# One attention and FFN block on one core: the rows of x are made again from their normalised form, and two kinds of transfer change queues

## The chip, the cores and the metric

The kernel runs on one core of a Trainium2 chip. The metric is device microseconds of one execution, the median of several runs. Before the change: median 1097.92 us of 3 runs, 1096.86 to 1098.83.

The engines are named as the profile names them: PE (TensorE, matrix products), DVE (VectorE), ACT (ScalarE), POOL (GpSimd) and SP (SyncE). SP computes nothing: it only issues transfers (DMAs). ACT and POOL can issue transfers too. Each engine works through its own instructions in the order in which the program gives them; one that waits holds up all that is behind it on that engine.

## The reference

```python
def attention(x, Wq, Wk, Wv, Wo):
    q, k, v = x @ Wq, x @ Wk, x @ Wv
    qT, kT, vT = (swapaxes(a, 1, 2) for a in (q, k, v))
    weights = softmax(qT @ swapaxes(kT, 1, 2) / sqrt(16))
    return swapaxes(weights @ vT, 1, 2) @ Wo

def ffn(x, lut, gate_idx, up_idx, down_idx):
    gate, up = x @ lut[gate_idx].T, x @ lut[up_idx].T
    return (silu(gate) * up) @ lut[down_idx].T

x = x + attention(layernorm(x), Wq, Wk, Wv, Wo)
x = x + ffn(layernorm(x), lut, gate_idx, up_idx, down_idx)
```

x is 2 x 2048 x 512, float32. The attention is over the 512 channels, not over the positions, so its weights are 512 x 512 for each of the two batches. The FFN's inner width is 1376; its three weights are indices into a table of 16 numbers. The layer norms have neither scale nor shift.

## The kernel before

The 4096 rows are cut into 8 chunks c of 512 rows, each into 4 blocks j of 128 rows (32 blocks k in all). A chunk of x lies in SBUF as tile `x{c}`, 128 partitions x 4 blocks x 512 channels, 1 MB. The order of work on PE, ACT, DVE and SP is the order in which the program is written out; helpers interleave the stages by hand.

1. Gram stage, up to 79.7 us. For each block, DVE computes the statistics (`stats`, L147), ACT takes the root (`sqrt`, L163), DVE the rest (`rest`), ACT writes the normalised block into a tile `xn` (`pair`, `normed`, L199), and PE adds its Gram matrix to `gp` (L396). `xn` holds two blocks and has two buffers. The normalised rows are also stored in DRAM as `nd`: chunks 3 to 7 from the `xn` pairs (`store`, L196, 10 stores of 512 KB), chunks 0 to 2 by a second pass of ACT into tiles `n` (`n_stored`, L493, 12 stores of 256 KB), which runs beside the Gram products of chunks 3, 5 and 6. SP issues all of them, and between them the loads of the weights wk and wq (L361, 1 MB each).
2. Small products, 79.7 to 176 us: the 512 x 512 matrices of the attention, with the softmax; they end in a matrix m for each batch.
3. The y stage, 176 to 289.5 us, one block k after the other (`y_product`, L709, 3.43 us each on PE). The rows needed for it are reloaded from `nd` in a turned layout (`n_load`, L688) and turned by DVE (`n_turned`, nT, L693). `side(k)` does what follows one product: `added(k-1)` adds y to x (L716), with sums on ACT (L158, L159); at a chunk's end the finished chunk of x is stored as `x1d` in DRAM (L722, 1 MB). `f_normed(k-6)` writes the second norm's rows into an `xn` pair, which `store` (L196) puts into DRAM as `xnd`. Every fourth block, `f_load` reloads a finished chunk of `xnd` into the room of the old x chunk (4 transfers of 256 KB, L688), and `f_turned(k-14)` lets DVE turn it into `xb` (L693). `f_sums` makes the sums that the fast products need (L128, L131).
4. Gate and up, 289.5 to 823.5 us: 44 units `GateUp(f, p)` of seven products each (L820), with copies by ACT (L849, L855, L860), silu by ACT (L872, L884), and adds by DVE. The last `added`, `f_normed`, turns and sums of stage 3 run here: `late` puts them into the list `todo`, one entry after each product. Between products DVE also looks up the FFN's weights (`pump`), whose indices POOL fetches (L271, L272, L304). The hidden rows are stored as `hd` (L843).
5. Down, 823.5 us to the end: 16 units `Down(h, jj)` of 16.85 us. Each loads its hidden rows (`Hidden`, L976, L982, 2.7 MB per chunk) and its two blocks of x (`r`, from `x1d`, L1018), adds the products to `r` (L131), and stores `r` as the output (L1047, L1085). The copies of products to SBUF are ACT's (L1055, L1062, L1068). A unit is created, and so its loads are issued, one unit ahead.

The index fetches are the only transfers that POOL issues. All others are SP's.

Of the kernel before, what the change touches and what calls it, by code (L numbers as in the profile page):

```python
# [40 lines left out]
F32 = mybir.dt.float32  # L44
# [3 lines left out]
AF = mybir.ActivationFunctionType  # L48
# [6 lines left out]
P = 128  # L55
# [6 lines left out]
def tile_attn_ffn(  # L62
# [13 lines left out]
    nc = tc.nc  # L76
    B, S, E = x.shape
    KB = E // P
    NLUT = lut.shape[1]
    INTER = down_idx.shape[0]  # L80
    J = 4
    CH = J * P
    NCH = B * S // CH
    CPB = S // CH
    NBLK = NCH * J
# [6 lines left out]
    Q = 32  # L92
# [10 lines left out]
    dram = ctx.enter_context(tc.tile_pool(name="dram", bufs=1, space=DRAM))  # L103
# [4 lines left out]
    eps_sb = const.tile([P, 1], F32, tag="eps", name="eps_sb")  # L108
    lut_i = lut_sb.bitcast(I32)
    wd = wdp.tile([P, NFT, E], F32, tag="wd", name="wd")  # L110
    x1d = dram.tile([NCH, P, J, E], F32, tag="x1d", name="x1d")
    nd = dram.tile([NCH, P, KB, J, P], F32, tag="nd", name="nd")
    xnd = dram.tile([NCH, P, KB, J, P], F32, tag="xnd", name="xnd")
    hd = dram.tile([NCH, NFT, P, CH], F32, tag="hd", name="hd")
# [4 lines left out]
    def room(tag, name):  # L119
        return keep.tile([P, J, E], F32, tag=tag, name=name)  # L120
# [11 lines left out]


    class Norm:
        def __init__(self, c, name):
            self.name = f"{name}{c}"
            self.rstd = const.tile([P, J], F32, tag=f"rstd_{self.name}", name=f"rstd_{self.name}")
            self.nmr = const.tile([P, J], F32, tag=f"nmr_{self.name}", name=f"nmr_{self.name}")
            self.minus, self.scale = -1.0, 1.0
# [25 lines left out]
        def rest(self, a, b):  # L165
            r0, q = self.r0[:, a:b], self.q[:, a:b]
            mean, var = self.mv[:, a:b, 0], self.mv[:, a:b, 1]
            rstd, nmr = self.rstd[:, a:b], self.nmr[:, a:b]
            stt = nc.vector.scalar_tensor_tensor
            nc.vector.reciprocal(r0, r0)  # L170

            if self.scale != 1.0:
                nc.vector.tensor_scalar_mul(var, var, self.scale)
            stt(q, var, EPS, r0, ALU.add, ALU.mult)
            stt(q, q, -0.5, r0, ALU.mult, ALU.mult)
            stt(rstd, q, 1.5, r0, ALU.add, ALU.mult)
            stt(nmr, mean, self.minus, rstd, ALU.mult, ALU.mult)

        def pair(self, j, block, quarters=False):


            if j % 2 == 0:
                self.xn = xnp.tile([P, KB, 2, P], F32, tag="xn", name=f"xn_{self.name}_{j}", bufs=2)
            to = self.xn[:, :, j % 2, :]
            if quarters:
                to = to.rearrange("p i (m a) -> p m i a", a=Q)
                block = block.rearrange("p (m i a) -> p m i a", i=KB, a=Q)
            else:
                block = block.rearrange("p (i e) -> p i e", i=KB)
            self.normed(j, block, to)  # L190
            return self.xn

        def store(self, j, dest):

            if j % 2:
                nc.sync.dma_start(dest[:, :, j - 1 : j + 1, :], self.xn)  # L196

        def normed(self, j, block, to):
            nc.scalar.activation(  # L199
# [137 lines left out]
    def pump(us):  # L337

        owed[0] = min(owed[0] + us, 2 * us + 1.0)
        while owed[0] > 0:  # L340
            cost = next(lookup, None)
            if cost is None:
                return
            owed[0] -= cost


    xc = [room(f"x{c}", f"x_{c}") for c in range(NCH)]
# [33 lines left out]


    ln1 = [Norm(c, "a") for c in range(NCH)]
    ln2 = [Norm(c, "f") for c in range(NCH)]
    gp = {}
    STORED = 3

# [101 lines left out]
    def n_stored():  # L489
        c, j = to_store.pop(0)  # L490
        t = sums.tile([P, E], F32, tag="e", name=f"n_{c}_{j}")
        ln1[c].normed(j, xc[c][:, j, :], t)
        nc.sync.dma_start(nd[c][:, :, j, :], t.rearrange("p (i e) -> p i e", i=KB))  # L493

    for c in range(1, NCH):
        for j in range(J):
# [180 lines left out]
    nls, nTs, ys, xfs, fls = {}, {}, {}, {}, {}  # L677
    xb, xs = {}, {}

    def block(k):  # L680
        return xc[k // J][:, k % J, :]

    def reload(t, rows):

        rows = rows.rearrange("(t b) i j e -> i b t (j e)", b=Q)
        t = t.rearrange("p t (j e) -> p t (j e)", e=P)
        for i in range(KB):
            nc.sync.dma_start(t[i * Q : (i + 1) * Q], rows[i])  # L688
        return t.rearrange("p t (j m a) -> p j m t a", j=J, a=Q)

    def turn(to, t):

        nc.vector.transpose(to.rearrange("p m (t b) -> p m t b", b=Q), t)  # L693

    N_AT = ("a0", "a1", "a0", "a1", "a2", "a3", "a1", "a3")

    def n_load(c):
        nls[c] = reload(room(N_AT[c], f"nl_{c}"), nd[c])

    def n_turned(k):  # L700
        if k < NBLK:
# [11 lines left out]
    def added(k):  # L713
        c, j = divmod(k, J)
        total = small.tile([P, 1], F32, tag="total", name=f"total_{k}")
        nc.vector.scalar_tensor_tensor(  # L716
            block(k), ys[k], 1.0, block(k), ALU.mult, ALU.add, accum_out=total
        )
        ln2[c].sums(j, total, block(k))
        if j == J - 1:  # L720
            ln2[c].sqrt(0, J)
            nc.sync.dma_start(x1d[c], xc[c])  # L722

    def f_normed(k):
        c, j = divmod(k, J)
        ln2[c].pair(j, block(k), quarters=True)
        ln2[c].store(j, xnd[c])
# [5 lines left out]
        return xb[c][:, :, j * P : (j + 1) * P]  # L733

    def f_load(c):
        fls[c] = reload(room(f"x{c}", f"fl_{c}"), xnd[c])

    def f_turned(k):
        turn(f_place(k), fls[k // J][:, k % J])
# [30 lines left out]
        [("sq1", 1), (f"x{NCH - 1}", 0), (f"x{NCH - 1}", 1)],  # L770
    ]

    def side(k):

        if k - 1 < NBLK:
            added(k - 1)
        if 0 <= k - 14 < NBLK and k < NBLK:
            f_turned(k - 14)
        if k % J == 1 and 0 <= (k - 5) // J < NCH:
            ln2[(k - 5) // J].rest(0, J)  # L780
        if 0 <= k - 6 < NBLK:
            f_normed(k - 6)
        if k % J == 3 and 0 <= (k - 11) // J < NCH:
            f_load((k - 11) // J)
        if 2 * J + 14 <= k < 2 * J + 18:
            next(f_pairs[0])

    f_pairs = {p: f_sums(p) for p in range(NPR)}
# [5 lines left out]
    for k in range(NBLK):  # L794
        if k:
            n_turned(k + 1)
        y_product(k)
        if k == 0:
            before[0].a4()
            n_turned(1)  # L800
            n_load(1)
        else:
            if k % J == 3 and k // J + 2 < NCH:
                n_load(k // J + 2)
            side(k)
        pump(1.4 if k < 14 else 0.7)
    pps.release()
    sums.release()
    ffn = tc.alloc_tile_pool(name="ffn", bufs=1, reuse_waits="tile")
# [116 lines left out]
            pump(1.0)  # L926


    def late(i, turned=None, pair=None):
        def ops():  # L930
            if i < 8:
                side(NBLK + i)
            if turned is not None:
                f_turned(turned)
            if pair is not None:
                next(f_pairs[pair])

        todo.append(ops)

    what = [dict(turned=k) for k in range(NBLK - 14, 5 * J)] + [dict(pair=1)] * 4  # L940
    what += [dict(turned=k) for k in range(5 * J, 6 * J)] + [dict(pair=2)] * 4
    what += [dict(turned=k) for k in range(6 * J, NBLK)] + [dict(pair=3)] * 4
    for i, w in enumerate(what):
        late(i, **w)

# [61 lines left out]
    class Down:  # L1007


        def __init__(self, h, jj):  # L1010
            self.h, self.c, self.jj, self.name = h, h.c, jj, f"{h.c}_{jj}"
            self.r = []
            if h.c % 2 == 0 and jj == 0:
                for q in range(2):
                    rows_in[q] = room(f"x{1 + q}", f"r_{h.c}_{q}")
            for i, j in enumerate((jj, 2 + jj)):
                t = rows_in[h.c % 2][:, 2 * jj + i, :]
                nc.sync.dma_start(t, x1d[h.c][:, j, :])  # L1018
                self.r.append(t)

        def at(self, a):
            return a[:, self.jj * P : (self.jj + 1) * P]
# [69 lines left out]
        def end(self):  # L1092
            pass

    rows_in = {}

    def by_two(ops):
        return [
# [4 lines left out]
    units = [(0, 0), (1, 0), (0, 1), (0, 2), (0, 3), (1, 1), (1, 2), (1, 3)]  # L1103
    units += [(f, p) for f in range(2, NFT) for p in range(NPR)]
    line = Line(between)
    for f, p in units:
# [3 lines left out]
        if f == NFT - 1 and p == 0:  # L1110
# [3 lines left out]
            for name in ("hp0", "dT"):  # L1114
                hps[name] = tc.alloc_tile_pool(
                    name=name, bufs=1, side="right", reuse_waits="tile"
                )
            hps[0] = hps["hp0"]
            h = Hidden(0)
# [4 lines left out]
        if f == NFT - 1 and p == 3:  # L1124
            units = [Down(h, 0)]
# [9 lines left out]
    for c in range(NCH):  # L1135
        nxt = None
        for jj in range(2):
            if c == 0 and jj == 0:
                line.flush()
                ffn.release()  # L1140
                wgu.release()
                hps[1] = tc.alloc_tile_pool(name="hp1", bufs=1, reuse_waits="tile")
                dtp = tc.alloc_tile_pool(name="dt", bufs=6, reuse_waits="tile")
            if jj == 0 and c + 1 < NCH:
                nxt = Hidden(c + 1)
                nxt.rest_of()
            u = units.pop(0)
            if jj == 0:
                units.append(Down(h, 1))
            elif nxt is not None:  # L1150
                units.append(Down(nxt, 0))
                todo += by_two(nxt.sums())
            line.run(u, final=nxt is None and jj == 1)
        for op in todo:
            op()
        todo.clear()
        h = nxt
# [52 lines left out]
```

## Time and profile before

| what | value |
|---|---|
| median of 3 runs | 1097.92 us |
| the profiled execution: its time | 1099.27 us |
| the profiled execution: its span, first to last instruction | 1096.7 us |
| mean granted clock of PE | 0.998 |
| moved by DMA | 125.51 MB, mean 114 GB/s |
| y stage window, 216 to 262 us | 13.06 MB, 284 GB/s |

The page's part 3 (queue, kind: packets, MB, share of 16 engines' span) and its part 6 (what is moved, by whose queue, how often, KB each, median us from the issue to the landing) tell who moves what:

```profile
q1 hardware_dynamic: 76320, 117.47, 34.1%
q0 software_dynamic: 2240, 7.41, 2.2%
...
nl<-nd SPq DMA_DIRECT2D x32, 256.0 KB, 6.3
x1d<-x SPq DMA_DIRECT2D x8, 1024.0 KB, 9.3
xnd<-xn_f SPq DMA_DIRECT2D x16, 512.0 KB, 6.8
fl<-xnd SPq DMA_DIRECT2D x32, 256.0 KB, 6.8
r<-x1d SPq DMA_DIRECT2D x32, 256.0 KB, 3.9
```

The q1 line is SP's queue; the q0 line is POOL's, with the index fetches alone. In a wait line, the engine and line that waited stand left of the arrow and what ended the wait stands right of it, followed by the us in total, the number of times and the longest.

### The profile page before, as it was taken

What the parts mean: (1) busy time and instruction counts of PE and PEld (TensorE: products, weight loads), DVE (VectorE), ACT (ScalarE), POOL (GpSimd) and SP (SyncE); (2) the same over time, 40 slices, a digit from 0 to 9 for tenths busy, and PEclk for the clock granted to TensorE, in tenths of its full rate; (3) what the DMA queues carried; (4) which work ended last, traced back from release to release, by engine and by line L of the source; (5) the groups of instructions that cost most, each with busy time, mean ns of one, the idle gap of its engine ahead of it and who ended that gap; (6) DMA issues with size and microseconds to landing.
All of it is one profiled execution on the core that took longest, in us unless ns stands there. A gap on an engine that the chain in (4) does not pass through costs nothing.

```text
span 1096.7 us, 10068 instructions
## 1 busy us (share of the span) xinstructions
PE 1086.0 (99%) x3460; PEld 649.2 (59%) x3460; DVE 709.7 (65%) x1340; ACT 295.9 (27%) x554; POOL 15.7 (1%) x34
## 2 busy tenths in 40 slices
PE   9999999999999999999999999999999999999998
PEld 5668886444434444444444444444338888888887
DVE  6977777877665787878888787763553334433341
ACT  4642532554522222222322222222221000000000
POOL 0000000000000000000000000000000000000000
PEclk9999999999999999999999999999999999999999
DMA  8571313799861111111111111111415544345521
GB/s 342 174 233 23 75 39 87 208 285 280 237 178 48 48 62 58 64 48 68 57 61 65 56 67 54 48 48 39 140 55 175 171 151 144 99 156 171 160 68 39
DMA packets 78610, 125.51 MB, mean 114 GB/s; under 512 B 14288, under 2 KB 34000, under 8 KB 76640
## 3 DMA queue, kind: packets, MB, share of 16 engines
q1 hardware_dynamic: 76320, 117.47, 34.1%
q0 software_dynamic: 2240, 7.41, 2.2%
q8 instruction: 27, 0.44, 0.2%
q14 instruction: 23, 0.19, 0.1%
HBM read 68.76 MB, written 56.10 MB: 114 GB/s over the span
## 4 chain that ended last, share of the span: by engine, by line
PE 90%; DMA 4%; DVE 3%; ACT 2%; SPq 1%; issue 1%; ACTq 0%; DVEq 0%
PE a_g L820 27%; PE a_d L820 14%; PE c_g L820 13%; PE c_d L820 7%; PE b_g L820 7%; PE y L709 6%; PE b_d L820 4%; PE gp L396 3%; DMA fl<-xnd 2%; PE ea_t L546 1%; PE ea_p L546 1%; PE ea_m L546 1%; PE ea_s L546 1%; DMA xnd<-xn_f 1%; DMA nd<-xn_a 1%; DVE st_a L147 1%
## 5 line engine op out<-in xcount | busy, mean ns | idle before, releaser
L709 PE MATMUL y<-m,nT 128*128 128x512 f32 x256 | 110.5, 593 | 1.5 <-DVE nT L693 1.5
L131 DVE TENSOR_TENSOR c<-c_g,u 128x512 f32<-128x512 f32 (+1 forms) x44 | 30.4, 690 | 121.0 <-PE c_g L820 110.2
L709 PEld LDWEIGHTS y<-m,nT 128*128 128x128 f32 x256 | 48.5, 190 | 62.4 <-issue 56.9
L820 PE MATMUL a_g<-xb,s 128*128 128x512 f32 (+1 forms) x176 | 82.8, 593 | 0.8 <-DVE c L131 0.8
L820 PE MATMUL a_g<-xb,w 128*128 128x512 f32 (+1 forms) x176 | 82.8, 593 | 0.0
L820 PE MATMUL c_g<-xb,w 128*128 128x512 f32 (+1 forms) x176 | 82.7, 592 | 0.0
L820 PE MATMUL b_g<-xb,w 128*128 128x512 f32 (+1 forms) x176 | 82.7, 592 | 0.0
L820 PE MATMUL a_g<-xT_a,s 128*128 128x512 f32 (+1 forms) x176 | 82.7, 592 | 0.0
L872 ACT ACTIVATE h<-h 128x512 f32<-128x512 f32 (+1 forms) x44 | 27.7, 630 | 163.2 <-DVE h L131 163.2
L396 PE MATMUL gp<-xn_a 128*128 128x512 f32 (+3 forms) x256 | 70.3, 435 | 1.0 <-ACT xn_a L199 1.0
L820 PE MATMUL a_g<-xT_sq,s 128*128 128x512 f32 (+1 forms) x132 | 63.4, 603 | 2.2 <-ACT p L849 2.2
L396 PEld LDWEIGHTS gp<-xn_a 128*128 128x128 f32 x256 | 44.2, 190 | 27.7 <-issue 15.5
L820 PEld LDWEIGHTS a_g<-xb,s 128*128 128x128 f32 (+1 forms) x176 | 32.9, 188 | 43.7 <-issue 37.7
L245 DVE TENSOR_SCALAR gu<-idx_gu,lut_x,lut_sb 128x1024 int32<-128x1024 int32 (+1 forms) x77 | 58.6, 794 | 0.0
L820 PEld LDWEIGHTS a_g<-xb,w 128*128 128x128 f32 (+1 forms) x176 | 32.9, 188 | 42.7 <-issue 42.0
L820 PEld LDWEIGHTS a_g<-xT_a,s 128*128 128x128 f32 (+1 forms) x176 | 33.0, 188 | 42.5 <-issue 42.5
L820 PEld LDWEIGHTS b_g<-xb,w 128*128 128x128 f32 (+1 forms) x176 | 33.0, 188 | 42.5 <-issue 42.5
L820 PEld LDWEIGHTS c_g<-xb,w 128*128 128x128 f32 (+1 forms) x176 | 33.0, 188 | 42.5 <-issue 42.3
L257 DVE COPY_PREDICATED gu<-b_gu,gu 128x1024 f32<-128x1024 int16 (+1 forms) x44 | 56.3, 1280 | 0.8
L820 PE MATMUL a_d<-dT,hs_a 128*128 128x256 f32 x224 | 56.2, 379 | 0.0
L257 DVE COPY_PREDICATED wd<-b_wd,wd 128x512 f32<-128x512 int16 (+2 forms) x63 | 54.1, 859 | 1.1
L131 DVE TENSOR_TENSOR r<-r,a_d 128x256 f32<-128x256 f32 x32 | 13.5, 421 | 54.0 <-PE a_d L820 54.0
(240 smaller groups left out, 1721.3 us busy)
## 6 DMA issues: line engine op xcount, KB each, us to landing
hd<-h SPq DMA_DIRECT2D x80, 256.0 KB, 2.0
h<-hd SPq DMA_DIRECT2D x40, 512.0 KB, 6.5
nl<-nd SPq DMA_DIRECT2D x32, 256.0 KB, 6.3
x1d<-x SPq DMA_DIRECT2D x8, 1024.0 KB, 9.3
xnd<-xn_f SPq DMA_DIRECT2D x16, 512.0 KB, 6.8
fl<-xnd SPq DMA_DIRECT2D x32, 256.0 KB, 6.8
r<-x1d SPq DMA_DIRECT2D x32, 256.0 KB, 3.9
out_dram<-r SPq DMA_DIRECT2D x31, 256.0 KB, 2.5
```

The lines of the kernel that those rows point to most:

```text
L131: nc.vector.tensor_tensor(dest, a, b, ALU.add)
L147: nc.vector.bn_stats(st, block)
L245: vec.tensor_scalar(dest.bitcast(I32), idx, lut_x[:rows, k : k + 1], lut_i[:rows, at : at + 1], ALU.bitwise_and, ALU.bitwise_xor,)
L257: vec.copy_predicated(dest, masks[level - 1], t)
L396: nc.tensor.matmul(gp[b][i][:, i * P :], xn[:, i, j % 2, :], xn[:, i:, j % 2, :], start=c % CPB == 0 and j == 0, stop=c % CPB == CPB - 1 a ...
L546: nc.tensor.matmul(ps[:, m, :], self.a[a][:, k, m * P : (m + 1) * P], self.b[b][:, k, :], start=first and m == k == 0, stop=k == 1, skip_g ...
L709: nc.tensor.matmul(ys[k], nTs[k][:, i, :], m[:, i, :], start=(i == 0), stop=(i == KB - 1))
L820: nc.tensor.matmul(ps, lhsT, rhs, start=first and i == 0, stop=i == len(pairs) - 1, skip_group_check=not first,)
L872: nc.scalar.activation(self.h0, self.h0, AF.Silu)
```

## The change

x with the attention added is no longer stored: `x1d` and its stores go. In the down stage the normalised rows `xnd`, which are in DRAM anyway, are loaded into a tile `xn_back`, and ACT makes x from them again, as normalised row x deviation + mean (`undone`). For that, `rest` of the second norm also writes 1/rstd and the mean, over the first norm's tiles (`back`). The stores of `nd` and `xnd` are issued by ACT instead of SP, and the reloads `fl` of `xnd` by POOL instead of SP; the reloads `nl` stay with SP. The turns `f_turned` come 16 blocks behind instead of 14, with what hangs on that number (the first pair's sums, the rate of `pump`, the list of late work, whose last slot for turns takes two).

```diff
     class Norm:
-        def __init__(self, c, name):
-            self.name = f"{name}{c}"
+        def __init__(self, c, name, back=None):
+            self.name, self.back = f"{name}{c}", back
+            if back:
+                self.std, self.mean = back.rstd, back.nmr
...
             stt(nmr, mean, self.minus, rstd, ALU.mult, ALU.mult)
+            if self.back:
+                nc.vector.reciprocal(self.std[:, a:b], rstd)
+                nc.vector.tensor_scalar_mul(self.mean[:, a:b], mean, -self.minus)
...
             if j % 2:
-                nc.sync.dma_start(dest[:, :, j - 1 : j + 1, :], self.xn)
+                nc.scalar.dma_start(dest[:, :, j - 1 : j + 1, :], self.xn)
+
+        def undone(self, j, xn, to):
+
+            nc.scalar.activation(
+                to.rearrange("p (m i a) -> p i m a", i=KB, a=Q),
+                xn.rearrange("p i (m a) -> p i m a", a=Q), AF.Identity,
+                bias=self.mean[:, j : j + 1], scale=self.std[:, j : j + 1],
+            )
...
-    ln2 = [Norm(c, "f") for c in range(NCH)]
+    ln2 = [Norm(c, "f", back=ln1[c]) for c in range(NCH)]
...
-        nc.sync.dma_start(nd[c][:, :, j, :], t.rearrange("p (i e) -> p i e", i=KB))
+        nc.scalar.dma_start(nd[c][:, :, j, :], t.rearrange("p (i e) -> p i e", i=KB))
...
-    def reload(t, rows):
+    def reload(t, rows, queue):
...
-            nc.sync.dma_start(t[i * Q : (i + 1) * Q], rows[i])
+            queue.dma_start(t[i * Q : (i + 1) * Q], rows[i])
...
-        nls[c] = reload(room(N_AT[c], f"nl_{c}"), nd[c])
+        nls[c] = reload(room(N_AT[c], f"nl_{c}"), nd[c], nc.sync)
...
             ln2[c].sqrt(0, J)
-            nc.sync.dma_start(x1d[c], xc[c])
...
-        fls[c] = reload(room(f"x{c}", f"fl_{c}"), xnd[c])
+        fls[c] = reload(room(f"x{c}", f"fl_{c}"), xnd[c], nc.gpsimd)
...
+    LAG = 16
+
     def side(k):
 
         if k - 1 < NBLK:
             added(k - 1)
-        if 0 <= k - 14 < NBLK and k < NBLK:
-            f_turned(k - 14)
+        if 0 <= k - LAG and k < NBLK:
+            f_turned(k - LAG)
...
-        if 2 * J + 14 <= k < 2 * J + 18:
+        if 0 <= k - LAG - 2 * J < 4:
             next(f_pairs[0])
...
-        pump(1.4 if k < 14 else 0.7)
+        pump(1.4 if k < LAG else 0.7)
...
-    what = [dict(turned=k) for k in range(NBLK - 14, 5 * J)] + [dict(pair=1)] * 4
-    what += [dict(turned=k) for k in range(5 * J, 6 * J)] + [dict(pair=2)] * 4
-    what += [dict(turned=k) for k in range(6 * J, NBLK)] + [dict(pair=3)] * 4
+    what = [dict(turned=[k]) for k in range(NBLK - LAG, 5 * J)] + [dict(pair=1)] * 4
+    what += [dict(turned=[k]) for k in range(5 * J, 6 * J)] + [dict(pair=2)] * 4
+    what += [dict(turned=[k]) for k in range(6 * J, NBLK - 2)]
+    what += [dict(turned=[NBLK - 2, NBLK - 1])] + [dict(pair=3)] * 4
...
+            if not normed_in:
+                normed_in.append(room("sq0", "xn_back"))
+            self.n = [normed_in[0][:, 2 * jj + i, :] for i in range(2)]
+            self.n = [t.rearrange("p (i e) -> p i e", i=KB) for t in self.n]
             for i, j in enumerate((jj, 2 + jj)):
-                t = rows_in[h.c % 2][:, 2 * jj + i, :]
-                nc.sync.dma_start(t, x1d[h.c][:, j, :])
-                self.r.append(t)
+                nc.sync.dma_start(self.n[i], xnd[h.c][:, :, j, :])
+                self.r.append(rows_in[h.c % 2][:, 2 * jj + i, :])
+
+        def rows(self):
+
+            for i, j in enumerate((self.jj, 2 + self.jj)):
+                ln2[self.c].undone(j, self.n[i], self.r[i])
...
             if c == 0 and jj == 0:
+                units[0].rows()
                 line.flush()
...
             line.run(u, final=nxt is None and jj == 1)
+            if units:
+                units[0].rows()
```

More of the change, by code (lines that the diff above doesn't have):

```diff
@@ L110, in tile_attn_ffn @@
     wd = wdp.tile([P, NFT, E], F32, tag="wd", name="wd")
-    x1d = dram.tile([NCH, P, J, E], F32, tag="x1d", name="x1d")
     nd = dram.tile([NCH, P, KB, J, P], F32, tag="nd", name="nd")
@@ L926, in between, with late @@
             pump(1.0)
-    def late(i, turned=None, pair=None):
+    def late(i, turned=(), pair=None):
         def ops():
@@ L932, in ops @@
                 side(NBLK + i)
-            if turned is not None:
-                f_turned(turned)
+            for k in turned:
+                f_turned(k)
             if pair is not None:
@@ L1093, in end @@
             pass
-    rows_in = {}
+    rows_in, normed_in = {}, []
     def by_two(ops):
```

## The prediction

> **What bounds the kernel now.** I read the page's first part, then TensorE's waits, then the timeline around each wait.
>
> ```profile
> PE 1086.0 (99%) x3460; PEld 649.2 (59%) x3460; DVE 709.7 (65%) x1340; ACT 295.9 (27%) x554; POOL 15.7 (1%) x34
> ...
> PE a_g L820 <- ACT p L849: 2.2, 1, 2.2
> PE y L709 <- DVE nT L693: 1.5, 1, 1.5
> PE idle L377 <- POOL ident masks.py:199: 1.4, 1, 1.4
> PE gp L396 <- ACT xn_a L199: 1.0, 2, 0.6
> PE a_g L820 <- DVE c L131: 0.8, 1, 0.8
> ```
>
> TensorE sets the time: 1086.0 of 1096.7 us. No matmul changes, so the change can only give or take idle time of TensorE, and all that is there to win is in these waits. Three of them end at a transfer that is late; the column in brackets is the idle time before the instruction and what ended it:
>
> ```profile
> 69.93 1.52 ACT L199 ACTIVATE xn_a<-x,nmr_a,rstd_a 128x512 f32<-128x512 f32 x2 [5.34 <-DMA nd<-xn_a]
> ...
> 259.19 0.71 DVE L693 STREAM_TRANSPOSE xb<-fl 128x512 f32<-128x512 f32 x1 [5.14 <-DMA fl<-xnd]
> ...
> 305.19 1.52 ACT L199 ACTIVATE xn_f<-x,nmr_f,rstd_f 128x512 f32<-128x512 f32 x2 [5.54 <-DMA xnd<-xn_f]
> ```
>
> At 69.93 ScalarE waits for a store to free its buffer and TensorE loses 0.59 us at 70.2. At 259.19 VectorE, in order, stands at a turn whose reload has not landed; nT behind it is late and TensorE loses 1.50 us. At 305.19 ScalarE waits for a store, the copy p (L849) behind it is late, and TensorE loses 2.19 us. Why that last store was late is seen on SP's queue:
>
> ```profile
> 291.69 2.57 SPq L688 DMA_DIRECT2D fl<-xnd  x4
> 294.36 0.38 SPq L722 DMA_DIRECT2D x1d<-x  x1
> 295.12 2.41 SPq L196 DMA_DIRECT2D xnd<-xn_f  x2
> ```
>
> It stands behind 1 MB of reload and 1 MB of x1d on one queue, and lands after 9.99 us by the chain of waits, where the same kind of store needed 3.6 us at best. The windows (TensorE busy, PEld, DVE, ACT, POOL, granted clock, DMA share, GB/s) show what the 2.19 us cost beyond themselves, and how full the transfers are in the y stage:
>
> ```profile
> 305.00:307.20 2.20, 0.04 (x1) 0.00 (x0) 0.00 (x0) 2.01 (x4) 0.00 (x0) 1.00 0.55 90
> 307.20:308.80 1.60, 1.57 (x3) 0.82 (x4) 0.00 (x0) 0.96 (x2) 0.00 (x0) 0.70 0.92 236
> 308.80:310.40 1.60, 1.60 (x3) 0.57 (x3) 0.00 (x0) 0.00 (x0) 0.00 (x0) 0.50 1.04 206
> 310.40:312.00 1.60, 1.60 (x4) 0.64 (x3) 0.00 (x0) 0.58 (x1) 0.00 (x0) 0.74 1.05 234
> ...
> 216.00:262.00 46.00, 44.50 (x104) 19.49 (x104) 33.58 (x84) 22.39 (x52) 1.06 (x2) 1.00 1.02 284
> ```
>
> The clock fell to 0.50 after the gap: 1.6 x (0.30 + 0.50 + 0.26) = 1.70 us lost. After the gaps of 0.59 and 1.50 us it stayed at 1.00.
>
> **Part 1: x1d goes, stores move to ScalarE, reloads to GpSimd (y stage, 176 to 310).** In 216 to 262 the engines of the DMA are full (1.02). Of 13.06 MB there, x1d is 3 MB; without it the share falls to about 0.8 (estimate by bytes), and a store no longer waits behind reloads in SP's order. The store at 295.12 then has at best 3.6, at worst some 6 us (the median of stores there was 7.4 with the queue full); it lands by 301, and p (L849) comes at about 303 instead of 306.62; TensorE wants it at 305.0. So 2.19 and 1.70 go. The reload of 250.26 (8.80 us) was issued at 248.15 because SP first waited for the next chunk's store; on POOL it waits only for its own chunk's second store (issued 238.76) and the index fetch ahead of it (244.80). Four issues of 0.54 (the fetch's row) and 7.6 us landing (the fetch's, in the same full window) give 255. It is wanted two blocks of 3.43 us later than before (LAG 16 for 14): 260 or later. So 1.50 goes. The cover of a reload is five blocks, 17.2 us; with three (10.3) it would be 1 to 4 us late, and nT after it.
>
> Queues passed: SP's loads nl no longer stand behind these stores, and its hd stores come nearer. POOL, busy 1%, gets 32 issues of 0.54 us, in order behind the fetches at 204.29 and 244.80, which wait for VectorE; the reloads behind them need stores that come later anyway. ScalarE gets 16 issues; it is busy 22.39 of 46 us there, 1.9 us per block of 3.43, and half a store per block (0.35) fits. VectorE gets 16 tiny operations (0.16 each, 2.6 us in all) and the same turns later; it idles 12 of those 46 us. The four pair sums (1.18) at blocks 24 to 27 make its blocks some 0.3 us too long each, within the block that nT runs ahead. Behind the y stage the list of late work grows from 26 to 27 entries, which just fills the 27 places ahead of the unit that reads the last sums; its first product needs none of them.
>
> Every POOL issue in the trace took 0.53 to 0.85 us, beside a VectorE that was 70% busy, so the sum goes by 0.54. A rule speaks against POOL: the Trainium skill, "SBUF — State Buffer", section "SBUF: two separate sides", says that GpSimd cannot write a transfer's descriptors while VectorE holds the port that the two share; its example has 0.62 us turned into 3.1. By that figure (an estimate) a reload's four issues would take 12.4 us, the reload would end some 3 us past its cover in each of eight chunks, and most of the 1.50 would stay. No issue of this trace shows such a delay.
>
> **Part 2: the 22 stores of nd on ScalarE (30 to 76).** No row shows a store issued by ScalarE. The nearest are SP's (issue ns, min/median/max):
>
> ```profile
> L493 SPq DMA_DIRECT2D nd<-n x12: 512/562/2704, 33.1 to 68.2; - x12
> ...
> L196 SPq DMA_DIRECT2D nd<-xn_a x10: 512/513/2202, 33.8 to 74.3; - x10
> ```
>
> SP starts two ready stores 0.70 us apart (55.61, 56.31), so I take 0.70 per store in ScalarE's order, which waits for the activation before it too. Behind each store stand the next xn and so TensorE. Chunk 3: xn(4,0) was ready at 42.15 and wanted at 43.55, lead 1.4. Six stores come before it; three fall into ScalarE's 2.90 us wait until 37.39, the other three cost 2.1: 0.7 late. Chunk 4's two fall into waits (0.98 and 1.21). Chunks 5 and 6: 16 activations of 0.705, 12 stores of 0.70, two roots of 0.2, copies of g 0.9: 21.0 us against TensorE's 17.5; the lead of 4.9 us less 0.8 for xn itself covers it. Sum 0.8 late. With 0.61 per issue (0.80 per store): chunk 3 adds 0.3, chunks 5 and 6 add 1.2 less the 0.5 of lead left: 1.8. Between the minimum 0.51 and what a median of 0.56 to 0.61 gives, I take 1.2. Lower end: 0, if issuing overlaps compute. Upper end: rival C. The 0.59 at 70.2 goes: that store (59.82, 9.93 us) stood behind wk and wq on SP's queue and now has its own.
>
> **Part 3: the down stage (823 on).** 32 activations, nearest row xn_f at 0.80: 1.5 us per unit, before p (L1055), which waits for TensorE anyway:
>
> ```profile
> 873.65 0.37 ACT L1055 COPY p_d<-a_d 128x256 f32<-128x256 f32 x1 [9.57 <-PE a_d L820]
> ```
>
> The worst load (issued 858.71 behind 2.7 MB of hidden rows) landed after 9.5 us, at 869.2. In 512-byte pieces add 1 us (nd<-n 4.4 against r<-x1d 3.9, both 256 KB, doubled): rows ready 871.8, before 873.65. If they come later, p is late, and then TensorE's a2 at 878.4: cover 6 us. First unit: 839.8 + 1.5 against 844.7. SP's 32 issues grow by 0.1 us, and it waits for VectorE and TensorE there. I cost it at 0.
>
> **Sum.** -0.59 - 1.50 - 2.19 - 1.70 + 1.2 = -4.8 us: span 1096.7 to 1091.9. The profiled run took 1099.27, 2.6 around its span and 1.35 above the median of the runs shown; it would take 1094.5, the median 1097.92 - 4.8 = 1093.1. What TensorE gains early is kept: from 320 to 820 it is busy without a gap and VectorE waits for it.
>
> A second page bears on the 1.70: "TensorE: Matmul & The Clock Gate", section "Part 1: The HAM clock gate", has the clock fall after about 3.4 us of idleness, which would leave 2.19 us unpunished. The row shows 0.50 after it; by the page the sum would be -3.1.
>
> **Rivals.** About 2.2 us (0.2%) is what a measurement of this kernel tells from no change.
> A, forecast: 1093.1, itself 1092 to 1095.5.
> B, issuing costs ScalarE nothing: 1097.92 - 6.0 = 1091.9. For it: ScalarE's compute and its queue might run apart. Against: each store waits for the activation just before it, so nothing is left to overlap.
> C, slower: ScalarE takes over SP's blocked issues. Behind wk and wq SP's issues took 1.05, 2.70, 2.05 and 2.20 us, mean 2.0, 1.5 over the minimum. Each such store among the twelve of chunks 5 and 6 adds 1.5 us once 0.5 of lead is gone. Six of them: 0.8 + 8.9 - 0.5 = 9.2, and 1097.92 - 6.0 + 9.2 = 1101.1; it decides from the sixth. For it: wk and wq still come then. Against: they stay in SP's queue, and ScalarE's holds stores alone.
> D, the waits stay: three queues share 16 full engines, the reload or the store is late again, and only the 0.59 goes: 1097.92 - 0.6 + 1.2 = 1098.5. For it: the share of 1.02. Against: 3 of 13 MB gone and two blocks more of cover.
>
> **How the numbers follow.** A 0.51, B 0.13, C 0.21, D 0.15. Faster: A and B, 0.64; same: D, 0.15; slower: C, 0.21. The range leaves out most of C and a little below B: 1090.9 to 1100.4.
>
> **What would show it.** TensorE's waits for p (L849) and nT gone; clock at 1.00 from 290 to 320; one new wait of under 1 us at a gp near 43.5 and small ones near 66 to 71; ScalarE's store issues at 0.5 us; VectorE not waiting for fl; the down stage without gaps. Wrong if issues on ScalarE exceed 1 us, if xb waits for fl, or if p (L1055) waits for xn_back.

## The result, and the profile after

The changed kernel takes 1093.45 us (median of 6 runs, 1093.19 to 1093.8); the kernel before, on the same chip, 1098.38 (6 runs, 1096.86 to 1099.03). The ratio is 0.9954, 95% interval 0.9943 to 0.9966. The forecast was 1093.1. The profiled execution took 1093.44 us with a span of 1091.3.

The first engine line of the page after, and TensorE's waits (engine and line that waited, what ended the wait: us in total, times, longest):

```profile
PE 1083.4 (99%) x3460; PEld 648.7 (59%) x3460; DVE 712.1 (65%) x1356; ACT 321.5 (29%) x586; POOL 33.3 (3%) x66
```

```profile
PE gp L411 <- ACT xn_a L214: 1.8, 5, 0.7
PE idle L392 <- POOL ident masks.py:199: 1.4, 1, 1.4
PE a_g L836 <- DVE c L133: 0.8, 1, 0.8
PE ea_s L561 <- ACT a L582: 0.3, 1, 0.3
```

The waits for p (2.2 before) and for nT (1.5) are gone. The wait of gp for xn_a has grown from 1.0 to 1.8 us. Two stretches of the prediction's windows follow as they are now, the y stage and what was the gap at 305 with its slow clock (the last three columns are the granted clock, the DMA share and GB/s):

```profile
216.00:262.00 46.00, 46.00 (x109) 20.34 (x108) 34.89 (x93) 24.48 (x58) 9.90 (x18) 1.00 0.89 225
...
305.00:307.20 2.20, 2.20 (x7) 1.00 (x6) 0.00 (x0) 0.58 (x1) 0.00 (x0) 1.00 0.95 319
307.20:308.80 1.60, 1.60 (x6) 0.64 (x5) 1.48 (x3) 0.00 (x0) 0.00 (x0) 1.00 0.18 57
308.80:310.40 1.60, 1.60 (x5) 0.73 (x4) 1.60 (x3) 0.56 (x1) 0.49 (x1) 1.00 0.46 169
```

TensorE is busy without a gap in both and the clock stays at 1.00. The share of the transfers fell from 1.02 to 0.89, not to the estimated 0.8, while the rate fell from 284 to 225 GB/s. On ScalarE around 300, the store of a pair of normalised rows, the next pair, and the copy p:

```profile
293.87 0.52 ACTq L203 DMA_DIRECT2D xnd<-xn_f  x1
...
298.85 1.51 ACT L214 ACTIVATE xn_f<-x,nmr_f,rstd_f 128x512 f32<-128x512 f32 x2
...
300.94 0.58 ACT L865 COPY p<-a_g 128x512 f32<-128x512 f32 x1 [0.59 <-PE a_g L836]
```

xn_f, which waited 5.54 us for a store here before, now waits for none in this stretch (its only wait for a store is 2.41 us at 244.62, and TensorE does not feel it); p starts 4 us before TensorE wanted it in the old profile (305.0). Four marks split the difference of the two spans: the first matmul of the squares (end of the gram stage), the first of gate and up, the first of the down stage, the end.

| stretch | before | after | difference | predicted |
|---|---|---|---|---|
| to the first ea_p (79.54, 80.22) | 79.54 | 80.22 | +0.68 | +0.61 (T5 1.2 less T1 0.59) |
| to the first a_g (289.32, 288.17) | 209.78 | 207.95 | -1.83 | -1.50 (T2) |
| to the first a_d (823.34, 817.92) | 534.02 | 529.75 | -4.27 | -3.89 (T3 2.19, T4 1.70) |
| to the end | 273.36 | 273.38 | 0.0 | 0 (part 3) |

T1 to T5 are the terms of the prediction's sum in its order: the stall at 70.2, the late nT, the late p, the slow clock, ScalarE's issues. These are two single executions, and the one of the kernel before had the slow clock. The gram stage shows where ScalarE's issues are felt. Three lines of ScalarE, then two of TensorE:

```profile
42.03 0.52 ACTq L508 DMA_DIRECT2D nd<-n  x1
42.59 1.04 ACT L234 CAST b_gu<-idx_gu 128x1024 int16<-128x1024 int32 x1 [0.59 <-ACT n L214]
43.54 1.51 ACT L214 ACTIVATE xn_a<-x,nmr_a,rstd_a 128x512 f32<-128x512 f32 x2
...
44.41 8.90 PE L411 MATMUL gp<-xn_a 128*128 128x512 f32 x32 [0.69 <-ACT xn_a L214]
71.48 5.01 PE L411 MATMUL gp<-xn_a 128*128 128x512 f32 x17 [0.26 <-ACT xn_a L214]
```

An issue takes 0.52 us, and the cast behind it starts 0.59 us after the end of the activation before. xn of chunk 4 is 0.69 us late at 44.41; the prediction had 0.7 near 43.5. SP's queue holds a surprise: wk and wq, which SP issued at 56.88 and 58.15 before, now go out right behind x, because no store stands before them in its order.

```profile
17.64 0.38 SPq L376 DMA_DIRECT2D wk_sb<-in_wk_dram  x1
18.29 2.76 SPq L376 DMA_DIRECT2D wq_sb<-in_wq_dram  x1
```

### The profile page after: what moved, and what is told of

Its sections match the earlier page's. It is cut to its first block, busy times and chain, and to the rows that moved or that the text cites. A ratio compares the mean times of both kernels' runs of the same rounds, so it can differ in the third digit from the quotient of the medians.

```text
span 1091.3 us, 10100 instructions
## 1 busy us (share of the span) xinstructions
PE 1083.4 (99%) x3460; PEld 648.7 (59%) x3460; DVE 712.1 (65%) x1356; ACT 321.5 (29%) x586; POOL 33.3 (3%) x66
## 4 chain that ended last, share of the span: by engine, by line
PE 93%; ACT 2%; DVE 2%; DMA 1%; ACTq 1%; issue 0%; SPq 0%; DVEq 0%
PE a_g L836 28%; PE a_d L836 14%; PE c_g L836 14%; PE y L724 10%; PE c_d L836 7%; PE b_g L836 7%; PE b_d L836 4%; PE gp L411 2%; PE ea_t L561 1%; PE ea_p L561 1%; PE ea_m L561 1%; ACT xn_a L214 1%; DMA x<-in_x_dram 1%; DVE st_a L151 1%; PE ea_s L561 1%; PE ec_t L561 1%
## 5 line engine op out<-in xcount | busy, mean ns | idle before, releaser
L865 ACT COPY p<-a_g 128x512 f32<-128x512 f32 (+1 forms) x44 | 25.7, 585 | 78.1 <-PE a_g L836 78.1
```

The costliest lines, as they stand in the source:

```text
L865: nc.scalar.copy(self.p1, self.a)
```

## The experiments

Each was timed over 5 to 11 runs. E1 to E12 edit the changed kernel. The kernel before, run beside them, had medians of 1097.35 (E1 to E4), 1097.87 (E5 to E8) and 1097.64 (E9 to E12). It scatters by up to 3.5 us within one group, the changed kernel by 0.6, so kernels are compared by their own medians. The changed kernel was not run again beside them, and the three groups ran on three chips: a difference from its 1093.45 is one between occasions. E3, E4 and E6, on two of these chips, come within 0.1 us of it.

**E1, the stores of nd back on SyncE.**

```diff
-        nc.scalar.dma_start(nd[c][:, :, j, :], ...)
+        nc.sync.dma_start(nd[c][:, :, j, :], ...)
...
-            ln1[c].store(j, nd[c])
+            ln1[c].store(j, nd[c], nc.sync)
```

> The changed kernel with the 22 stores of nd issued by SyncE again; the stores of xnd stay on ScalarE, the reloads on GpSimd. Theory (term T5: the stores cost 0.70 us each in ScalarE's order and delay xn and TensorE in the gram stage): the stalls of 0.69 us at 44.4 and of about 0.7 us between 48 and 72 go; wk and wq stand behind the stores on SP's queue again, so the 0.59 us near 70 come back. The gram stage ends at 79.7 instead of 80.4, the median falls by 0.7 us against the changed kernel, to 1092.8. Rival (issuing on ScalarE is free there, the new stalls have another cause, as in the smaller pieces of the lookup): the stall at 44.4 stays, and with the 0.59 back the median is 1093.5 to 1094.1.

Measured 1092.96 (1092.79 to 1093.3). The stall at 44 is gone, and the one near 70 is back, larger than the old 0.59:

```profile
71.01 8.90 PE L411 MATMUL gp<-xn_a 128*128 128x512 f32 x32 [0.97 <-ACT xn_a L214]
```

The first theory's signs hold. The gain is 0.5 instead of 0.7; the returning stall is larger than the one that was priced.

**E2, the same, and wk and wq loaded right behind x.**

```diff
+    wk_sb = load_weight(wk, "a0", "wk_sb")
+    wq_sb = load_weight(wq, "a1", "wq_sb")
     nc.gpsimd.memset(eps_sb, EPS)
```

> As the run before, and wk and wq are loaded right behind x, ahead of every store of nd on SP's queue. Theory: neither ScalarE's issues (0.7 net of the 0.59 in the changed kernel) nor the 2 MB of weights in front of a store are left, the gram stage ends at 79.1, the median is 1092.2, and this is the fastest of all. Rival (the 0.59 at 70 is not from wk and wq standing in front of the store at 59.8): the stall near 70 stays, median 1092.8.

Measured 1091.81 (1091.6 to 1092.27; ratio 0.9951, 0.9938 to 0.9965). The windows from 40 to 80, of E2 and then of the changed kernel (the second number is TensorE's busy time):

```profile
40.00:80.00 40.00, 40.00 (x156) 26.02 (x155) 34.68 (x71) 23.54 (x40) 0.85 (x1) 1.00 0.63 197
```

```profile
40.00:80.00 40.00, 39.06 (x148) 24.75 (x146) 32.51 (x69) 24.62 (x39) 0.85 (x1) 1.00 0.63 197
```

No gap is left. In E2 and the changed kernel wk and wq leave at the same time (17.43 and 17.64), so the two differ in who issues the stores of nd: 1093.45 - 1091.81 = 1.64 us is what ScalarE's issues cost (T5, priced at 1.2). The two profiles agree: the first ea_p starts at 78.60 and at 80.22. E1 and E2 differ in when the weights are loaded: 1.15 us (T1, priced at 0.59).

**E3 and E4, the stores of xnd, or the reloads fl, back on SyncE.**

```diff
-        ln2[c].store(j, xnd[c])
+        ln2[c].store(j, xnd[c], nc.sync)
```

> The changed kernel with the 16 stores of xnd issued by SyncE again. Theory (the 2.19 and 1.70 us at 305 came from the 2 MB of reload and x1d that stood in front of the store on one queue; both are gone from SP's queue whoever issues the store): TensorE does not wait for p, clock 1.00 in 305 to 312, median 1093.4, within 0.4 us of the changed kernel. Rival (a queue of ScalarE's own is what made the store land early): the store near 293 to 295 lands after over 8 us, TensorE waits for p again, median 1095 to 1097.

```diff
-        fls[c] = reload(room(f"x{c}", f"fl_{c}"), xnd[c], nc.gpsimd)
+        fls[c] = reload(room(f"x{c}", f"fl_{c}"), xnd[c], nc.sync)
```

> The changed kernel with the reloads fl issued by SyncE again; the stores stay on ScalarE. Theory (fl was late in the kernel before for want of cover and for SP's order behind x1d and the stores; with 16 blocks of lag and the others gone SP does as well): no wait of VectorE for fl, median 1093.4, within 0.4 us of the changed kernel. Rival (SP's order alone makes fl late: it waits there for the store's landing, and the loads nl stand behind it): nT or xb late by 1 to 3 us, median 1094.4 to 1096.4.

Measured 1093.45 (1093.15 to 1093.8) and 1093.51 (1093.12 to 1093.79): the changed kernel's time both times. TensorE waits for neither p nor nT. In E4 VectorE waited for a reload once, 1.3 us, which the theory had not expected and TensorE did not feel. Each rival falls; with x1d gone neither move is needed by itself.

**E5, LAG 14.**

```diff
-    LAG = 16
+    LAG = 14
```

> The changed kernel with LAG back at 14: a reload is wanted three blocks (10.3 us) after it is issued, as before, instead of five. Theory (the queues and the missing x1d made the reload early enough, the two blocks more are spare): by the changed kernel's rows the last of four issues comes at 1.7 us and the pieces land in 6.2 to 7.2 us more, 8.9 at most; VectorE waits for fl hardly at all, TensorE for no nT, median 1093.4, within 0.4 us of the changed kernel. Rival (the prediction's figure: with three blocks the reload is 1 to 4 us late): VectorE waits for fl several times, TensorE waits for nT as in the kernel before, median 1094.4 to 1096.

Measured 1093.12 (1092.88 to 1093.5). TensorE waits for nT nowhere, and VectorE waits for fl once, 1.0 us. With x1d gone the two more blocks are spare. (Its span is the changed kernel's, 1091.3; the 0.3 us lie outside the span and were not explained.)

**E6, the stores of x1d added again.**

```diff
             ln2[c].sqrt(0, J)
+            nc.sync.dma_start(x1d[c], xc[c])
```

> The changed kernel with the eight stores of x1d (1 MB each, on SP's queue) added again, which nothing reads; all else stays changed. Theory (what made p and nT late was one queue's order: reload and x1d in front of a store): the transfers fill up to a share of 1.0 again in 216 to 262, but store and reload have their own queues, TensorE waits for neither p nor nT, median 1093.4 to 1093.9. Rival (the 16 engines being full is what made them late, on whatever queue): p waits near 305 or nT near 260 again, some of 1.50 + 2.19 + 1.70 us comes back, median 1095 to 1098.

Nothing reads x1d here. Measured 1093.53: four runs of 1093.12 to 1093.78, one of 1095.53, which was not explained. In 262 to 290 the transfers are nearly full again (in 216 to 262 the share is 0.92, not the expected 1.0). xn_f waits for its stores four times, 7.3 us in all, once at 300.78, and VectorE waits for two reloads:

```profile
262.00:290.00 28.00, 28.00 (x66) 12.35 (x65) 20.69 (x51) 14.13 (x34) 4.44 (x9) 1.00 0.95 285
```

```profile
300.78 1.52 ACT L215 ACTIVATE xn_f<-x,nmr_f,rstd_f 128x512 f32<-128x512 f32 x2 [2.06 <-DMA xnd<-xn_f]
...
DVE xb L709 <- DMA fl<-xnd: 3.0, 2, 1.8
```

TensorE loses nothing: 28.00 of 28.00, and p comes in time. For p, then, nearly full transfers alone are not enough; the store that was 9.99 us on its way behind reload and x1d is what made it late. For nT E6 shows less. The reload that came late before, issued at 248.15, leaves at 251.15 on GpSimd's queue, and VectorE still waits 1.20 us for it although it wants it two blocks (6.9 us) later. With 14 blocks it would have been some 8 us late (an estimate, 1.20 + 6.86). So with x1d on the way it is the two blocks that kept nT in time and not the other queue; x1d with 14 blocks and the new queues was not run.

**E7, E8 and E12, the weights held back.** E7 and E12 let ScalarE write one element of each weight's room, which SyncE's loads must wait for; E8 issues the loads from ScalarE.

```diff
+                for tag in ("a0", "a1"):
+                    nc.scalar.copy(room(tag, f"{tag}_held")[:, 0, 0:1], eps_sb)
                 wk_sb = load_weight(wk, "a0", "wk_sb")
                 wq_sb = load_weight(wq, "a1", "wq_sb")
```

> The changed kernel with wk and wq held back to where the kernel before issued them (about 57 us): ScalarE first writes one element of each room there, SyncE's loads wait for that; two copies of about 0.2 us are added to ScalarE. This is rival C of the prediction with its condition filled: 2 MB on the way while ScalarE issues the last ten stores of nd. Theory (a blocked issue is a matter of its own queue): ScalarE's stores still take 0.51 to 0.58 us, the gram stage ends 0.2 to 0.6 us later than in the changed kernel, median 1093.6 to 1094.1. Rival C (any 2 MB on the way block an issue): stores of 1 to 2.7 us on ScalarE, median 1096 to 1102.

Measured 1097.11 (1095.1 to 1097.83, 11 runs). The loads went out at 60.81, later than meant. The windows around the new stall:

```profile
70.00:71.70 1.70, 1.60 (x7) 0.95 (x5) 1.63 (x4) 0.46 (x1) 0.00 (x0) 1.00 1.10 372
71.70:73.50 1.80, 0.00 (x0) 0.00 (x0) 1.80 (x5) 0.80 (x2) 0.00 (x0) 1.00 1.13 364
73.50:75.10 1.60, 1.54 (x4) 0.93 (x5) 1.60 (x5) 0.72 (x2) 0.00 (x0) 0.93 0.97 314
75.10:76.70 1.60, 1.60 (x5) 1.12 (x5) 1.60 (x3) 1.16 (x2) 0.00 (x0) 0.50 0.83 278
76.70:78.30 1.60, 1.60 (x4) 0.70 (x3) 1.56 (x3) 0.36 (x1) 0.00 (x0) 0.50 0.20 67
```

TensorE stands 1.96 us, and then runs at half its clock, which costs 1.6 x (0.07 + 0.50 + 0.50) = 1.7 us, as after the 2.19 us before. Eight of the 11 runs have a mean clock of 0.998 (median 1097.28), three 1.000 (median 1095.15): the slow clock is worth 2.1 us and does not come every time. The price is in C's range but hardly by C's mechanism: two issues are longer (0.73 and 1.02), the rest 0.52, 0.7 us more in all. What ended the wait of xn in front of the stall (2.23 us) the profile takes for a VectorE step on the weights, which xn does not read; a store that freed its buffer late, as in E8 and E12, is the likelier cause, but here it is not shown.

```diff
-                wk_sb = load_weight(wk, "a0", "wk_sb")
+                wk_sb = load_weight(wk, "a0", "wk_sb", nc.scalar)
```

> The changed kernel with wk and wq issued by ScalarE, in its order where the kernel before had them (about 57 us), so that they stand in front of the last ten stores of nd on ScalarE's own queue. Theory (a queue with 2 MB in front of it blocks the issues behind): as on SP before, four to six stores take 1 to 2.7 us, xn and TensorE behind them are late by 4 to 9 us, median 1098 to 1102.5. Rival (only SyncE's issues block, ScalarE hands its work over): stores stay at 0.5 us, the two loads cost 0.4 us each, median 1093.8 to 1094.5.

Measured 1095.52 (1095.17 to 1096.01), between the two expectations. All stores take 0.52 to 0.58 us, so the queue's own 2 MB do not block ScalarE's issues; but the store issued at 64.68 lands after 7.63 us and xn waits for its buffer.

E12 is E7 with the copies one step earlier, behind xn of chunk 5, block 2, so that the loads leave at 56.27, where the kernel before had them.

> The changed kernel with wk and wq held back to 56.6 us, where the kernel before issued them (56.9); when they were held back to 60.8 they cost 3.7 us. Theory (stores and weights share the 16 DMA engines whatever their queues: the store of xn_a issued near 63.5 lands after 6 to 8 us instead of 3.2 and frees its buffer late): TensorE loses 0.5 to 1.5 us at about 71, clock stays at 1.00, median 1093.9 to 1095. Rival (the prediction's first step: the store was late for standing behind the weights in SP's queue, and ScalarE's own queue frees it of them): the store lands in 3 to 4.5 us, median 1093.3 to 1093.8.

Measured 1095.37 (1095.08 to 1096.01). Part of its chain of waits (start, us, what), and TensorE's gaps:

```profile
57.65 0.82 ACT xn_a L214
58.47 0.02 issue
58.49 8.49 DMA nd<-xn_a
66.98 0.02 issue
```

```profile
67.93 4.58 PE L411 MATMUL gp<-xn_a 128*128 128x512 f32 x16 [0.98 <-ACT xn_a L214]
72.95 8.90 PE L411 MATMUL gp<-xn_a 128*128 128x512 f32 x32 [0.44 <-ACT xn_a L214]
```

The store at 58.49 is on ScalarE's queue, the weights are on SyncE's, and it takes 8.49 us all the same (3.2 in the median of the changed kernel). The rival, which was the prediction's own step, falls: a queue of its own does not protect a store from 2 MB on the way. The median, 1095.37, is above the range of either expectation (1093.9 to 1095 and 1093.3 to 1093.8).

**E9, each store of nd in two halves.**

```diff
+        for i in (0, 2):
+            nc.scalar.dma_start(nd[c][:, i : i + 2, j, :], t[:, i : i + 2, :])
```

> The changed kernel with each of the 22 stores of nd split into two issues of half the size on ScalarE: the same bytes in the same pieces, 22 issues more. Theory (an issue costs ScalarE about 0.57 us in its order whatever it moves, and ScalarE, with some 3 us idle left between 30 and 76, sets the end of the gram stage): 12.5 us more, less 2 to 3 of idle: the gram stage ends some 10 us later, median 1101 to 1105. Rival (the cost goes by the pieces, half an issue costs half): 22 times 0.05 us more, median 1093.5 to 1095.

Measured 1100.16 (1099.71 to 1101.52; ratio 1.0024, 1.0014 to 1.0033). The group of the halves in E9, and of whole stores in the changed kernel (issue ns, min/median/max):

```profile
L411 ACTq DMA_DIRECT2D nd<-xn_a x20: 366/424/491, 35.2 to 82.0; - x20
```

```profile
L508 ACTq DMA_DIRECT2D nd<-n x12: 520/521/576, 33.2 to 70.0; - x12
```

Half the bytes still take 0.42 of 0.52 us, and a pair of halves 0.89. So 22 pairs cost 22 x 0.37 = 8.1 us more, and 6.7 of them appear in the time. Both expectations miss, the first (1101 to 1105) less than the second (1093.5 to 1095): the cost goes mostly by the issue, and ScalarE's order does set the gram stage.

**E10, x1d gone alone**: the stores and reloads on SyncE and LAG 14, by the edits of E1, E3, E4 and E5 together.

> The part of the change that gives it its name, alone: x1d is not stored and the down product's rows are made from xnd, but every store and reload is on SyncE as before, and LAG is 14. Theory (x1d in SP's queue was enough to make p and nT late; the other queues and the two blocks are spare): no wait for p or nT, clock 1.00 in 305 to 312, the stall near 70 as before (0.6 to 1.0 us), median 1092.6 to 1093.4. Rival (SP's order of reload and stores makes them late without x1d too): nT waits near 260 or p near 305, median 1094.5 to 1097.

Measured 1092.72 (1092.56 to 1093.94): no more than the whole change takes. SP's queue, VectorE's and ScalarE's longest waits there, and the y stage window:

```profile
289.61 2.53 SPq L703 DMA_DIRECT2D fl<-xnd  x4
293.95 2.41 SPq L203 DMA_DIRECT2D xnd<-xn_f  x2
...
285.88 0.71 DVE L708 STREAM_TRANSPOSE xb<-fl 128x512 f32<-128x512 f32 x1 [3.59 <-DMA fl<-xnd]
...
300.01 1.52 ACT L214 ACTIVATE xn_f<-x,nmr_f,rstd_f 128x512 f32<-128x512 f32 x2 [1.53 <-DMA xnd<-xn_f]
...
216.00:262.00 46.00, 46.00 (x108) 20.33 (x107) 35.90 (x93) 23.70 (x56) 1.06 (x2) 1.00 1.00 236
```

The reload still stands in front of the store, but no x1d does; xn_f waits 1.53 us instead of 5.54. VectorE waits for reloads four times, 10.1 us in all (16.6 before), and none of this reaches TensorE. The reload that made nT late leaves no earlier than before (248.36 against 248.15), but VectorE waits 2.67 us for it instead of 5.14. The transfers are still full in this window (1.00, though at 236 GB/s instead of 284), so a full share by itself does not bring the waits. The old stall near 70 is there (1.11 us).

**E11, E10 with the weights loaded right behind x**, by the two lines of E2.

> As the run before, and wk and wq are loaded right behind x. Theory (these two things are all that is to be had): the stall near 70 goes too, median 1091.5 to 1092, as fast as the fastest of the earlier runs. Rival (with everything on one queue something is late again): 1092.5 or more, with a wait of TensorE in 216 to 312.

Measured 1091.98 (1091.66 to 1092.15; ratio 0.9944, 0.9932 to 0.9957). E2 and E11 beat both kernels: some 1.5 us below the changed one, with ranges that do not touch its own.

## Why the prediction was right, and where it was not

**T3, the late p: right, by a cause that two remedies meet.** The cause named was SP's order, with reload and x1d ahead of a store. Without x1d the store comes early enough on that one queue (E10); with x1d it comes early enough once stores and reloads have other queues (E6). The change does both, so half of it is spare here.

**T2, the late nT: the amount came, the step only in part.** The prediction had the reload issued earlier, off SP's order, and wanted two blocks later; in the changed kernel it leaves at 246.48 instead of 248.15. Taking x1d away is enough (E10), and there the reload is issued as late as before and only lands sooner. The queue by itself did not bring it earlier in E6; there the two blocks of lag did the work. What 14 blocks were said to cost, a reload 1 to 4 us late, showed once in E5 (1.0 us), with x1d gone.

**Rival D, that 16 full engines keep the waits, falls.** In E10 the share is still 1.00 in 216 to 262 and TensorE waits for neither p nor nT. The share did not follow the bytes either: 3 of 13 MB less gave 0.89 in the changed kernel, not 0.8.

**T1, the stall at 70.2: the amount came, the step was wrong.** The prediction said that the store "stood behind wk and wq on SP's queue and now has its own". E12 has the store on its own queue and the weights at the old time: it lands after 8.49 us and TensorE loses 0.98 and 0.44. The stall went because the weights moved from 57 to 18 us when SP lost its stores, which neither the forecast nor rival C saw ("wk and wq still come then"). The amount was luck. The early weights are worth 1095.37 - 1093.45 = 1.9 us in the changed kernel, some of it the two small copies that hold the weights; with SyncE's stores they are worth 1.15 (E1 to E2) and 0.74 (E10 to E11). Without this unforeseen move the time would have been about 1095.4 (an estimate, E12's), still inside the range.

**T5, ScalarE's issues: right mechanism, mis-sized.** Priced at 1.2 between 0 and rival C, measured 1.64 (E2). The price of 0.70 per store in ScalarE's order held: with a store between them two activations of the changed kernel start 1.41 us apart (33.81 and 35.22), without one 0.71. But it was read off the wrong thing. The two stores of the kernel before that were called ready were not; each leaves SP 0.03 us after its activation has ended on ScalarE (54.78 + 0.80 = 55.58, and 55.48 + 0.80 = 56.28):

```profile
54.78 0.80 ACT L199 ACTIVATE xn_a<-x,nmr_a,rstd_a 128x512 f32<-128x512 f32 x1
55.48 0.80 ACT L199 ACTIVATE n<-x,nmr_a,rstd_a 128x512 f32<-128x512 f32 x1
...
55.61 0.51 SPq L196 DMA_DIRECT2D nd<-xn_a  x1
56.31 0.51 SPq L493 DMA_DIRECT2D nd<-n  x1
```

So the 0.70 between them is the pace of the activations and not what an issue costs; that the two figures are equal was luck. Rival B, issues for free, falls with E2 and E9.

**What the sum left out: a wait cost TensorE more than the idle time shown.** Take the stretch from the gram products behind the small gt products (52.70 in E2) to the first ea_p (78.60 in E2). It takes 25.90 us in E2 and in E11, where no wait is shown in it. It takes 26.42 in the changed kernel with one wait of 0.26, 26.76 in the kernel before with one of 0.59, 27.14 in E1 with one of 0.97, 27.28 in E10 with one of 1.11, and 27.85 in E12 with two, 0.98 and 0.44. That is the wait shown and some 0.27 us more for each. In an unbroken run a product starts before the one ahead of it has ended, as here in E2 (77.62 + 1.14 = 78.76):

```profile
77.62 1.14 PE L414 MATMUL gp<-xn_a 128*128 128x384 f32 x5
78.60 1.89 PE L562 MATMUL ea_p<-wk_sb,g 128*128 128x256 f32 x8
```

Idle time counts from that end, so a wait loses the overlap too; whether this is all of the 0.27 was not tried. So T1 was 0.86 us and not 0.59, and T2 and T3 look short by as much: the table's rows have 0.33 and 0.38 us more than their terms.

**Rival C falls on both counts.** Its condition did not come, and where E12 and E8 made it come, issues of 0.52 to 0.77 us took the place of its 1.05 to 2.70; the loss was 1.9 to 2.1 us, through buffers freed late, not 9.2. E7, with the weights at 60.81, had one issue of 1.02 and lost 3.7, the slow clock included.

**T4, the slow clock: real in the profiled execution, mis-sized for the median.** The sum took 1.70 us off the median. Of 47 further runs of the kernel before, only four have a mean clock of 0.998 as its profiled execution had, and these take 1098.87 to 1099.93; the median of the others is 1097.53. So the 1.70 was in the profile (part of the 4.27 of the table) but in few of these runs. Against the others' median span of 1095.0 us the changed kernel gains 3.7, as the table gives without T4: 0.68 - 1.83 - (4.27 - 1.70) = -3.72. Measured so, the forecast of the median came out because three smaller things made up most of it: the y stage and the end at p gave 0.7 more than T2 and T3, probably the cost per wait that the sum left out; what lies around the span shrank from 2.5 to 2.1; and the 1097.92 it started from was 0.4 above the usual. The last two were luck. The six runs that the result stands on have no clock on record. Three of them took 1098.83 to 1099.03, so the slow clock may have been in up to half of them; against their median the gain is 4.9 us, next to the 4.8 forecast.

**Part 3, the down stage at no cost: right.** 273.36 and 273.38 us. The loads do come late, and ScalarE waits for them; TensorE does not:

```profile
ACT p_d L1080 <- PE a_d L836: 89.1, 16, 8.2
...
ACT r L207 <- DMA xn_back<-xnd: 33.8, 8, 7.4
```

p_d still waits for TensorE, all 16 times: the 33.8 us of waiting lie inside the cover of 6 us per unit. What if the cover were gone was not tried.

**GpSimd's issues: right.** The four issues of a reload take 2.21 us (0.55 each) with VectorE busy 34.89 of 46 us. "SBUF — State Buffer", section "SBUF: two separate sides", of the Trainium skill has a transfer issued from GpSimd go from about 0.62 to 3.1 us beside a VectorE copy that holds the port the two share. Such a lock was not seen here; no run shows whether VectorE had an operation of that kind in this window.

## What to carry to other kernels

A store that is moved off a queue moves everything behind it on that queue forward: list what comes earlier, not only what is moved, and ask what large load will then share the engines with whom. Before a wait in the profile is put into the sum, ask whether the median run has it: a profiled execution 1.35 us above the median had a slow clock that only four of 47 later runs had. Before two operations are timed by their distance, ask whether the second was ready or still waiting for its input. Where an edit holds several remedies for one wait, try each alone; here the removal of 8 MB of stores on its own gave all of it, and moving the stores of nd gave a new cost on an engine that sets the pace of its stage, and the early weights that it brought along can be had without it (E2, E11).

## What the runs showed of the hardware

After gaps of about 2 us TensorE's clock sometimes fell to half for some 3.4 us (1.7 us lost) and sometimes not: in the profiles after 2.19 us (before) and 1.96 us (E7) it did, after 2.02 us (E9) it did not; after gaps of 1.57 us and less it never did. In four of E9's ten runs the mean clock is 0.997 or 0.998, so there too it is not the same each time.

```profile
43.90:46.00 2.10, 0.07 (x2) 0.01 (x1) 1.13 (x3) 1.82 (x3) 0.00 (x0) 1.00 0.48 133
46.00:47.60 1.60, 1.60 (x4) 0.86 (x5) 0.00 (x0) 0.65 (x1) 0.00 (x0) 1.00 0.01 4
```

This is E9: no work for 2.02 us, then full clock. "TensorE: Matmul & The Clock Gate", section "Part 1: The HAM clock gate", of the Trainium skill asks for about 3.4 us of idleness; both slow stretches here followed less. Halving an issue of 0.52 us left 0.42. What lies around the span is 2.5 us in the kernel before, 2.1 in the changed one and 1.8 in E5 and E6; why was not found.
